# Two Mamba layers: C of every pair of states by DMA and a ScalarE copy to PSUM, where TensorE spread it from the rows of dbl

## The chip, the cores and the metric

The kernel runs on one core of a Trainium2 chip. The core's engines work side by side, each through its own list of instructions in order, and wait for each other by semaphores: TensorE (PE, with its weight loads as PEld), VectorE (DVE), ScalarE (ACT), GpSimd (POOL) and SyncE (SP), which here only issues DMAs. SBUF is the working memory of 128 partitions; PSUM holds what TensorE writes, and ScalarE and VectorE read and write it too. The metric is the time of one execution on the device, in microseconds (us), as the median of several executions.

## The reference

The network has four layers on x of shape (2, 128, 56, 56), each of them x + layer(group norm of x): an agent attention, a 3x3 convolution, a mixture of experts on 2x2 patches, and last a pair of Mamba blocks, one along each image row from left to right (f), one from right to left (b). The change lies in the Mamba blocks. Cut to what matters here:

```python
xz = x @ in_w.T;  xi, z = split(xz)                  # 256 channels each
xc = silu(conv_b + causal conv of xi with 4 taps)
dbl = xc @ xproj_w.T
dt, Bm, Cm = split(dbl, [8, 8 + 16])                 # 16 states
dt = softplus(dt @ dt_w.T + dt_b);  A = -exp(Alog)
# along the row, for every channel d and state s:
h[d, s] = exp(dt[d] * A[d, s]) * h[d, s] + dt[d] * xc[d] * Bm[s]
y[d] = sum over s of h[d, s] * Cm[s]
y = (y + xc * Dp) * silu(z);  result = y @ out_w.T
```

Both results are fused by one more matrix and normalized over the channels.

## The kernel before

The first three layers take the time up to about 1735 us and are not touched. The Mamba stage, `mamba_pair`, works on 14 blocks of 448 positions (8 image rows): 2 images, 7 blocks each. A block has two halves, f then b, and a half has 16 units. States go in pairs: pair j holds states 2j and 2j+1 in the lower and the upper 64 partitions. A pair has two units, m = 0 and 1, for the two groups of 128 channels; a unit holds its 128 channels as two runs r of 448 side by side, so that a tile is 128 partitions by 896. One unit consists of

- `decay`: two ScalarE activations write dA = exp(dt * A) to PSUM (L1820; two buffers);
- `push`: one GpSimd product, dBu = dtu * B (L1831; four buffers);
- `scan`: one VectorE scan along the rows, h = dA * h + dBu (L1853). After the second unit of a pair, one product over both units multiplies h by C, in place;
- `collect`: TensorE adds the two states of a pair into y with a matrix of two identities (L1873).

The product by C is done by GpSimd for the pairs 0, 3 and 6 of f and 0 and 3 of b (`POOLED`, L1440; the product is L1859), and by VectorE for the eleven others (L1862). Where GpSimd does it, C comes from SBUF: `send_low` writes the rows of B and C of a half (`low`, 40 rows: 8 of dt, 16 of B, 16 of C) to a DRAM buffer `far` and reads them back spread over 64 partitions each, B for all pairs (`Bs`) and C for the pooled pairs (`Cs`, one tile per direction). Where VectorE does it, `read_out` lets TensorE spread C: a column of the identity, broadcast to 64 columns, picks one row of `low` and writes it to 64 partitions of `c_ps`, a PSUM bank with the tag "c" of which there is one. Each of the two matmuls stands in the profile as two records, so a pair has four (L1841).

The order of the work is written out by hand. `units` lists all 448 units; the loop over them is a step each. In step n it issues `decay` of unit n+1; the fetches that were left by earlier stages (ScalarE copies out of PSUM); `push` of unit n+3; `scan` of unit n; `close` of a finished half (L1879, yv = y * silu(z)); `read_out` in the first unit of a pair that isn't pooled; `collect` of unit n-3, mostly; and then the stages that `book` put on this step: everything that prepares the next block (norm, conv, Silu, low, dt, softplus, weigh, the sends, the gates) and finishes the last one (fuse, the norm's statistics in `measure`, root, newton, normalize, turn_back, onto). A stage writes the bank "mm", or "c" where it is booked with that tag: f.low at step 15 of f, f.softplus(0) at step 6 of b, both softplus of b at the first two steps of the next f, conv(1) of b at step 12 of f. Places that the prediction speaks of, by their step n of a block (0 to 15 is f, 16 to 31 is b): the f Silu of the next block with the Silu of the gates at 10, the b Silu at 18 (two table loads and two activations each, L1884 to L1887), f.low at 15, b.send_steps at 11, f.send_steps at 27, fuse at 4, measure at 6.

The SP queue carries, in the order of the steps, `far`, `Bs`, `Cs`, the doubled copies `dtu` and `dt` of a half (`send_steps`, eight DMAs, L1808), and the result (L1688). `weigh` on GpSimd (L1793) makes dtu = dt * xc.

```python
units[0][0].decay(0)
for h, u in units[:3]:
    h.push(u)
for n, (h, u) in enumerate(units):
    if n + 1 < len(units):
        who, i = units[n + 1]
        who.decay(i)
    fetch(n)
    ...
```

## Time and profile before

| | |
|---|---|
| median of 5 executions | 3106.36 us (3105.32 to 3116.91) |
| profiled execution | 3105.2 us, span 3103.5 us |
| granted clock of TensorE, mean | 0.937 |
| Mamba stage, about 1735 us to the end | 1370 us |
| one block in its steady part | 95.2 us |
| L1831 dBu, GpSimd | 448 times 2140 ns |
| L1853 scan, VectorE | 448 times 2007 ns |
| L1862 product by C, VectorE | 154 times 2022 ns |
| L1859 product by C, GpSimd | 70 times 3991 ns |
| L1820 dA, ScalarE | 896 times 637 ns |
| L1841 c_ps, TensorE | 616 records, 172.9 us |
| L1873 y, TensorE | 1792 records, 469.1 us |
| Cs by DMA | 140 of 112 KB |

Times in the profile count from the start of the span. "PE" busy is modelled, since matmuls overlap; "PEclk" is the share of its full clock that TensorE was granted. A line of the timeline gives start, length, engine, source line, operation, output and inputs, how many instructions are merged into it, and in brackets the idle time before it and what ended it. A line of waits gives who waited for whom: total us, how often, the longest. A line of stretches gives, for each engine, its busy time with the number of instructions.

### The profile page before, as it was taken

The numbers are of one execution on the slowest core, as the hardware profiler recorded it, in microseconds if no ns is written. First come the engines' busy times: TensorE is split into PE (matmuls) and PEld (weight loads), VectorE is DVE, ScalarE is ACT, GpSimd is POOL, SyncE is SP. The second block draws the span as 40 slices with busy tenths as digits, with TensorE's granted clock in tenths as the row PEclk, the third lists the DMA queues.
The fourth block names the chain that finished last, engine by engine and source line by source line (L and its number), as shares of the span: only waits on it lengthen the run. The fifth ranks groups of instructions, "written<-read, shape, count | busy, mean of one in ns | idle before, by whom it ended". The sixth has DMA issues, their size and how long they took to land. (4 is left out here: it accounts for less than half of the span.)

```text
span 3103.5 us, 34608 instructions
## 1 busy us (share of the span) xinstructions
PE 2822.2 (91%) x12964; PEld 1076.8 (35%) x12964; DVE 2225.2 (72%) x2033; ACT 1758.6 (57%) x2634; POOL 1499.9 (48%) x801
## 2 busy tenths in 40 slices
PE   7999999999998899999996789999889998889885
PEld 3333333332344444444443322333323333233321
DVE  5879999999886111111112699999999999999996
ACT  5778788877641011111111577776777767777763
POOL 3000100100521000000002699999999999999995
PEclk9999999999998899999997888989989899999987
DMA  1000000000011878777773553444444535444440
GB/s 54 1 1 1 1 1 1 1 1 1 1 38 42 316 280 321 288 311 305 296 311 104 116 101 81 91 105 91 98 85 83 111 81 114 90 83 91 96 100 8
DMA packets 133271, 333.65 MB, mean 108 GB/s; under 512 B 20228, under 2 KB 90340, under 8 KB 129492
## 3 DMA queue, kind: packets, MB, share of 16 engines
q1 hardware_dynamic: 111104, 303.96, 34.0%
q0 software_dynamic: 5520, 15.62, 1.6%
q10 hardware_dynamic: 16452, 11.61, 1.2%
q8 instruction: 106, 1.74, 0.2%
q14 instruction: 89, 0.73, 0.1%
HBM read 262.56 MB, written 17.20 MB: 90 GB/s over the span
## 5 line engine op out<-in xcount | busy, mean ns | idle before, releaser
L1831 POOL TENSOR_TENSOR dBu<-dtu,Bs 128x896 f32<-128x896 f32 x448 | 944.9, 2140 | 50.9 <-DVE h L1853 38.1
L1853 DVE TENSOR_TENSOR_SCAN h<-dA,dBu 128x896 f32<-128x896 f32 x448 | 879.0, 2007 | 58.8 <-ACT dA L1820 46.2
L620 ACT ACTIVATE ex<-sc 128x896 f32<-128x896 f32 (+1 forms) x700 | 602.7, 917 | 124.6 <-PE sc L617 113.4
L627 DVE TENSOR_TENSOR ex_sum<-ex_sum,ex 128x1792 f32<-128x1792 f32 (+1 forms) x238 | 492.5, 2069 | 35.3 <-ACT ex L620 21.3
L1873 PE MATMUL y<-h,both 128*64 128x448 f32 x1792 | 469.1, 625 | 16.2 <-POOL h L1859 15.0
L617 PE MATMUL sc<-q,k 32*128 32x448 f32 (+1 forms) x2800 | 403.6, 587 | 3.6 <-ACT ex L620 2.9
L1341 PE MATMUL h_ps<-w,xs_c 128*128 128x512 f32 x896 | 393.0, 597 | 10.3 <-issue 10.3
L1820 ACT ACTIVATE dA<-dt,f_A 128x448 f32<-128x448 f32 x448 | 284.5, 637 | 107.1 <-DVE h L1853 76.4
L635 PE MATMUL av<-ex,va 128*32 128x448 f32 (+1 forms) x2800 | 334.3, 552 | 0.1
L1862 DVE TENSOR_TENSOR h<-h,c_ps 128x1792 f32<-128x1792 f32 x154 | 311.3, 2022 | 26.4 <-PE c_ps L1841 11.6
L582 POOL TENSOR_TENSOR a_e<-a_e,a_inv 112x784 f32<-112x784 f32 x14 | 41.6, 2973 | 583.9 <-ACT ex L620 394.5
L1820 ACT ACTIVATE dA<-dt,b_A 128x448 f32<-128x448 f32 x448 | 283.8, 636 | 66.8 <-DVE h L1853 53.6
L1345 DVE TENSOR_TENSOR he<-h_ps,sg 128x512 f32<-128x512 f32 x56 | 38.5, 691 | 381.4 <-PE h_ps L1341 344.4
L1289 POOL DMA_INDIRECT xr<-xd,whom x28 | 28.1, 1003 | 535.4 <-PE xr_ps L1331 489.7
L1859 POOL TENSOR_TENSOR h<-h,Cs 128x1792 f32<-128x1792 f32 x70 | 279.3, 3991 | 2.2 <-DVE h L1853 2.2
L1841 PE MATMUL c_ps<-low,ident 40*64 40x448 f32 x616 | 172.9, 642 | 89.6 <-DVE h L1862 67.4
L1341 PEld LDWEIGHTS h_ps<-w,xs_c 128*128 128x128 f32 x896 | 168.9, 191 | 218.3 <-issue 202.6
L1873 PEld LDWEIGHTS y<-h,both 128*64 128x64 f32 x1792 | 116.6, 150 | 319.8 <-issue 249.1
L617 PEld LDWEIGHTS sc<-q,k 32*128 32x128 f32 (+1 forms) x2800 | 137.7, 181 | 230.0 <-issue 132.3
L1362 PE MATMUL o_ps<-w,ht 128*128 128x512 f32 x448 | 197.2, 592 | 0.4 <-ACT ht L1357 0.4
L1344 ACT ACTIVATE sg<-h_ps 128x512 f32<-128x512 f32 x56 | 33.4, 597 | 256.5 <-PE h_ps L1341 256.5
L1364 ACT ACTIVATE ot<-o_ps,share 128x512 f32<-128x512 f32 x28 | 19.3, 688 | 278.9 <-PE o_ps L1362 278.9
(334 smaller groups left out, 3059.5 us busy)
## 6 DMA issues: line engine op xcount, KB each, us to landing
w<-in_L_conv_w_dram SPq DMA_DIRECT2D x28, 4096.0 KB, 19.3
w<-in_L_conv_w_dram SPq DMA_DIRECT2D x28, 2048.0 KB, 10.3
Bs<-far SPq DMA_DIRECT2D x56, 896.0 KB, 10.6
dtu<-sp_u SPq DMA_DIRECT2D x108, 224.0 KB, 3.9
dt<-dt SPq DMA_DIRECT2D x108, 224.0 KB, 5.2
Cs<-far SPq DMA_DIRECT2D x140, 112.0 KB, 7.5
os<-ot ACTq DMA_DIRECT2D x28, 256.0 KB, 7.8
xd<-xt SPq DMA_DIRECT2D x14, 224.0 KB, 2.8
```

Of the source, the lines that this page charges most:

```text
L617: nc.tensor.matmul(sc[:size, j, :BLK], self.m.k[rows, at : at + size], self.q[rows, :], start=True, stop=True)
L620: nc.scalar.activation(ex[:size, 2 * g : 2 * g + 2, :], sc[:size, :, :BLK], AF.Exp, scale=scale)
L627: nc.vector.tensor_add(self.total[g][:size], self.total[g][:size], ex[:size])
L635: nc.tensor.matmul(self.av[rows, :BLK], self.m.va[:size, i, rows], self.ex[i][:size, h, :], start=i == 0, stop=i == STEPS - 1,)
L1341: nc.tensor.matmul(h_ps, xc[:, q, :], w1[:, q, f0 : f0 + 512], start=q == 0, stop=q == 3)
L1362: nc.tensor.matmul(o_ps, ht[:, i, :], w2[:, i, :], start=i == 0, stop=i == nj - 1)
L1820: nc.scalar.activation(self.dA[u][:, r * BLK : (r + 1) * BLK], self.dt2[:, m, r, :], AF.Exp, scale=self.w.A[:, j, 2 * m + r : 2 * m + r + 1],)
L1831: nc.gpsimd.tensor_tensor(self.dBu[u], self.dtu2[:, m], self.B[:, j, :].unsqueeze(1).to_broadcast(shape), ALU.mult)
L1853: nc.vector.tensor_tensor_scan(hf, af, bf, 0.0, ALU.mult, ALU.add)
L1859: nc.gpsimd.tensor_tensor(h4, h4, c, ALU.mult)
L1862: nc.vector.tensor_tensor(h4, h4, c, ALU.mult)
L1873: nc.tensor.matmul(self.y[r * H : (r + 1) * H, m, :BLK], both, self.hc[j][:, m, r, :], start=False, stop=j == PAIRS - 1)
```

## The change

C comes by DMA for every pair, not only for the pooled ones. `send_low` sends B alone. A new `send_c(j)` sends C of one pair into a tile of 128 by 448, of which five rotate for both directions together; it is called six units ahead of use, and for the first three pairs before the loop. `read_out` is one ScalarE copy of that tile to `c_ps` in place of TensorE's matmuls, and it stands earlier in the step: after the fetches, before `push`, `scan` and the booked stages. GpSimd's product reads the pair's tile in place of a slice of the old one.

```diff
-                self.C = work.tile([P, len(pooled), BLK], F32, name="Cs", tag=f"Cs{self.w.d}", bufs=1)
                 for s in range(2):
                     half = slice(s * H, (s + 1) * H)
                     src = far[:S, :].rearrange("(j s) t -> s j t", s=2)
                     nc.sync.dma_start(self.B[half], src[s].unsqueeze(0).to_broadcast([H, PAIRS, BLK]))
-                    for n, j in enumerate(pooled):
-                        r = S + 2 * j + s
-                        nc.sync.dma_start(self.C[half, n, :], far[r : r + 1, :].to_broadcast([H, BLK]))
+            def send_c(self, j):
+                self.C[j] = work.tile([P, BLK], F32, name="Cs", tag="Cs", bufs=5)
+                for s in range(2):
+                    r = S + 2 * j + s
+                    nc.sync.dma_start(
+                        self.C[j][s * H : (s + 1) * H, :], self.far[r : r + 1, :].to_broadcast([H, BLK])
+                    )
...
             def read_out(self, u):
-                r = R + S + u // 2 * 2
                 self.c_ps = ps.tile([P, 512], F32, name="c_ps", tag="c")
-                for s in range(2):
-                    one_row = net.ident[:LOW, r + s : r + s + 1].to_broadcast([LOW, H])
-                    nc.tensor.matmul(self.c_ps[s * H : (s + 1) * H, :BLK], one_row, self.lo, start=True, stop=True)
+                nc.scalar.copy(self.c_ps[:, :BLK], self.C[u // 2])
...
+            for h, u in units[:6:2]:
+                h.send_c(u // 2)
             units[0][0].decay(0)
             for h, u in units[:3]:
                 h.push(u)
...
                 fetch(n)
+                if u % 2 == 0 and not h.by_pool(u):
+                    h.read_out(u)
+                if u % 2 == 0 and n + 6 < len(units):
+                    who, i = units[n + 6]
+                    who.send_c(i // 2)
                 if n + 3 < len(units):
                     who, i = units[n + 3]
                     who.push(i)
                 h.scan(u)
                 if done:
                     done.pop().close()
-                if u % 2 == 0 and not h.by_pool(u):
-                    h.read_out(u)
```

## The prediction

> **What bounds the kernel now.** I read the page's busy shares and slices first: the change lies in the last stage, the Mamba layers, from about 1735 us on. Then the busy times of that stage alone.

> ```profile
> PE 2822.2 (91%) x12964; PEld 1076.8 (35%) x12964; DVE 2225.2 (72%) x2033; ACT 1758.6 (57%) x2634; POOL 1499.9 (48%) x801
> ```

> ```profile
> 1800.00:3000.00 1200.00, 1082.68 (x3700) 370.15 (x3696) 1132.70 (x776) 879.51 (x1449) 1161.37 (x529) 0.91 0.46 94
> ```

> The second line's columns after the length are PE, PEld, VectorE, ScalarE, GpSimd, the granted clock, the DMA share and GB/s. VectorE is busy 94% and GpSimd 97%, so little can be won. Which of the two sets the pace is told by the waits of that stage:

> ```profile
> DVE h L1853 <- ACT dA L1820: 41.0, 38, 2.0
> DVE h L1862 <- PE c_ps L1841: 6.1, 13, 0.9
> DVE sp_e L1775 <- ACT dt_ps L1769: 2.8, 6, 1.3
> ...
> DVE h L1853 <- POOL dBu L1831: 0.6, 1, 0.6
> ```

> ```profile
> POOL dBu L1831 <- DVE h L1853: 31.8, 34, 2.2
> ```

> VectorE waits for GpSimd once; GpSimd waits for VectorE 34 times. So VectorE paces, and its waits for ScalarE and TensorE are the time that can change. A block takes 95.2 us (the residual adds of L1686 start at 2320.28, 2415.46 and 2510.93), and there are 13 blocks in which the next one is prepared. The timeline puts VectorE's waits at fixed places of each block: 0.2 to 0.9 before the first product of the f half (for c_ps), 0.84 at the f Silu, 1.98 at the b Silu, about 0.5 before b's last pair. The largest, on ScalarE and then VectorE:

> ```profile
> 2465.19 0.53 ACT L1735 COPY low<-low_ps 40x448 f32<-40x448 f32 x1 [1.26 <-PE low_ps L1732]
> 2465.62 1.30 ACT L1820 ACTIVATE dA<-dt,b_A 128x448 f32<-128x448 f32 x2
> ...
> 2470.34 0.55 ACT L1769 ACTIVATE dt_ps<-sp_e 128x448 f32<-128x448 f32 x1
> 2470.91 1.28 ACT L1884 ACT_TABLE_LOAD   x1
> ...
> 2475.30 1.31 ACT L1820 ACTIVATE dA<-dt,b_A 128x448 f32<-128x448 f32 x2
> ```

> ```profile
> 2476.71 3.94 DVE L1853 TENSOR_TENSOR_SCAN h<-dA,dBu 128x896 f32<-128x896 f32 x2 [1.98 <-ACT dA L1820]
> ```

> From the copy of low at 2465.19 to dA at 2475.30 ScalarE runs without a pause, so whatever comes into that chain, or delays its head, is paid in full. The head is TensorE's low_ps, which starts when VectorE's product of pair 7 (2461.38 to 2463.40) frees the bank "c".

> ```profile
> 2400.86:2404.27 3.41, 2.19 (x8) 0.56 (x10) 3.31 (x3) 3.23 (x7) 3.35 (x3) 1.00 0.14 31
> 2404.27:2407.68 3.41, 3.41 (x12) 0.77 (x8) 3.41 (x3) 0.93 (x2) 3.41 (x3) 0.50 1.01 234
> ...
> 2465.71:2469.12 3.41, 3.13 (x15) 1.08 (x14) 3.41 (x3) 3.34 (x7) 3.41 (x3) 1.00 0.20 25
> 2469.12:2472.53 3.41, 1.32 (x8) 0.20 (x4) 3.31 (x3) 3.35 (x6) 3.41 (x2) 1.00 1.00 222
> ```

> The clock fell after the first and the fourth, not after the third. If each matmul's time is weighted with its contracted rows over 128 (8 for dt_ps, 40 for c_ps, else about 128), the first has 0.30 of a window, the fourth 0.31, the third 0.54. Over all windows of the stage that began at full clock, every one up to 0.47 was followed by half clock and none from 0.48; from half clock it rose again from 0.81 on, never at 0.79 or less.

> [...] The window that ends at 2404.27 held 2.19 us of matmuls, so the trace decides for a load limit.

> **The change, part by part.** Removed: 308 matmuls of c_ps, 616 records, 0.90 us of TensorE per pair. Added: 154 ScalarE copies, and Cs by 448 DMAs in place of 140, 34 MB more.

> *VectorE and GpSimd* run the same instructions; their products stay at 2.02 and 3.99 us. Nothing.

> *The price of a copy.* SBUF to PSUM, 128x448: between the copy of low (next instruction 0.43 after it starts) and L1769 (0.55). I take 0.45. The copy waits for the product of the pair before (bank "c") and for two DMAs; behind it on ScalarE stand the step's later stages and the next dA, for which VectorE's scan waits. That dA waits anyway for a scan which comes after the same product. Eleven copies per block; ScalarE is idle 27% of the stage, and behind nine of them the next dA has a pause or at least 1.4 us before its scan. Two stand in the Silu chains:

> - b Silu, pair 1: in the unbroken chain above. +0.45 x 13 = +5.9. Its own product at 2471.18 then starts 0.3 later, hidden under the longer wait for dA.
> - f Silu, pair 5: before, ScalarE took xc at 2351.69 only when TensorE's conv was done, and Silu began at 2352.34. Without c_ps of pair 4 the conv ends 0.9 earlier; the copy then waits for the product that ends at 2351.34, and Silu begins at about 2351.95. -0.4 x 13 = -5.2.

> *First product of the f half.* c_ps was ready 1.07 after the dt copy that freed its bank; the ScalarE copy is ready 0.45 after it. The 13 waits of 6.1 in sum vanish: -6.1. The dt_ps waits (2.8) shrink, since TensorE no longer stops for c_ps ahead of dt_ps: -2.0.

> *Start of the stage.* Six Cs DMAs (0.67 MB) stood ahead of the first dtu and dt while the DMA engines were 99% busy at 211 GB/s, 3.2 us; now they follow. The first Silu can come 2.0 earlier (it is then held by conv_ps, done at 1735.15, where xc was taken at 1737.22). Next, 1.75 of c_ps ahead of dt_ps goes out of VectorE's wait of 1.99 for dt_ps: 1.7. At the first f Silu the conv comes 0.9 earlier and the copy costs 0.45: 0.5. Bounds 0 and -6; I take the sum, -4.2.

> *SP.* The send of pair b0 reuses the buffer of f3, and so waits for GpSimd's product (2440.44 to 2444.43). Behind it in the queue is b's send_steps, until now issued at 2438.16. It moves to 2445.7 (two issues, 1.27): dtu is issued by 2448.5, lands after 3.9, and is wanted at 2455.61; the last dt, issued about 2450.7, lands after 5.2, at 2455.9, and dA wants it at 2459.40. Cover 3.5 us or more: nothing. If a dt took the 11.8 of the slowest Cs, it would cost 3.1 a block, 40 in all. Copies have their Cs 17 us ahead of use against landings of 7.4. f's send_steps has the send of f0 ahead of it, released by GpSimd's product at 2396.2, 6 us before its own start at 2402.49. The 34 MB raise the stage's DMA share from 0.46 to some 0.6.

> *TensorE's clock.* With c_ps gone its work closes up and leaves longer pauses. Ahead of low_ps (lines of 2459 on):

> ```profile
> 2459.40 0.97 PE L1841 MATMUL c_ps<-low,ident 40*64 40x448 f32 x4 [1.00 <-ACT xc L1712]
> 2460.30 0.97 PE L1873 MATMUL y<-h,both 128*64 128x448 f32 x4
> 2461.20 1.03 PE L1720 MATMUL gate_ps<-pad,b_gate_t 128*128 128x448 f32 x2
> 2462.16 0.97 PE L1873 MATMUL y<-h,both 128*64 128x448 f32 x4
> 2463.46 1.32 PE L1732 MATMUL low_ps<-xc,f_xp_t 128*40 128x448 f32 x3 [0.32 <-DVE h L1862]
> ```

> The y and gate ahead now start at 2456 and end by 2458.9; the y of 2462.16 needs GpSimd's product, done at 2461.69. That is 2.8 us of nothing, and 0.6 more before low_ps. Nearly every position of the grid then has a window under 0.475 that ends between 2460.7 and 2464.0, so low_ps runs partly at half clock. It took 1.67 at full clock (2486.28) and 3.21 at half (1740.15). Bounds 0 and +1.54; I take 1.1, as the half clock begins or ends inside it: +14.3.

> The second place is between sp_ps and f's skip: without the two c_ps near 2425 and 2428 there are pauses of 1.9 and 1.0 with one gate (0.95) between. About half of the positions fall under the limit, and skip, fuse and conv then run late by 1.2 to 2.9 us. The norm's statistics on VectorE have 0.75 of margin behind fuse, and conv ends just in time for Silu. Bounds 0 and +2.7 a block; I take 0.78 as the mean: +10.1.

> [...]

> Sum: -4.2 - 6.1 - 5.2 - 2.0 + 5.9 + 14.3 + 10.1 = +12.8. The profiled execution took 3105.2 (span 3103.5), so 3118; the median shown, 3106.4, lies 1.2 above it.

> **The rivals.**

> *The clock holds.* If the last two terms are nothing, the sum is -11.6: 3094, faster. It decides at 0.475 of a window: TensorE's own work would have to stay spread out as now. For it: low_ps never ran at half clock before. Against it: c_ps itself weighs only 0.08 of a window, but its waits are what spread the rest.

> *Half of it.* low_ps slows, skip does not, or the other way: +2.7 or -1.5, about 3104 to 3108. Within 0.2% (6.2 us), which is about what can be told from no change.

> *A late transfer or a crowded ScalarE.* dt behind the queue on SP, up to +40 as above; or the copies cost 0.45 not twice but four to six times a block, +12 to +23. 3130 to 3158. Against it: the cover shown.

> **How the numbers follow.** Forecast 0.52, its own range 3111 to 3135. Clock holds 0.24, half of it 0.13, late transfer or crowded ScalarE 0.11. Faster 0.24, same 0.13, slower 0.52 + 0.11 = 0.63. The range goes from the clock rival's 3094, less 2, to 3140; below lies about half of that rival's spread, 0.1, above most of the last one.

> **What would show it.** Right: VectorE's wait at the b Silu grows from 1.98 to about 3.5, low_ps shows matmuls of about 1 us, the granted clock of the stage falls under 0.91, no wait for c_ps is left, the f Silu wait is about 0.5 in the blocks where skip is fast. Wrong: if low_ps stays at 0.54 a matmul, the sum falls to the first rival; if ScalarE or GpSimd waits for Cs or dt, to the last.

## The result, and the profile after

The changed kernel takes 3114.14 us (median of 26 executions, 3106.93 to 3120.47); the kernel before, run beside it, 3109.32 us (median of 50). The ratio is 1.0014, with a 95% interval of 1.0008 to 1.0021: slower, by about 4.4 us. The forecast was slower by 12.8. The profiled execution took 3109.71 us, with a span of 3107.9.

Line numbers move with the diff: dA is now L1822, the copy to c_ps L1840, the scan L1852, the product by C on VectorE L1861 and on GpSimd L1858, skip L1868, y L1872, the b Silu L1883 to L1886.

The busy times of the page, and the stretch from 1800 to 3000 us (PE, PEld, VectorE, ScalarE, GpSimd, granted clock, DMA share, GB/s):

```profile
PE 2685.4 (86%) x12348; PEld 1057.9 (34%) x12348; DVE 2225.5 (72%) x2033; ACT 1824.8 (59%) x2788; POOL 1499.2 (48%) x801
```

```profile
1800.00:3000.00 1200.00, 957.69 (x3131) 351.24 (x3132) 1128.65 (x773) 935.90 (x1583) 1155.01 (x526) 0.88 0.54 119
```

TensorE has 125 us less to do in this stretch, ScalarE 56 more, and the granted clock went from 0.91 to 0.88: TensorE does less and is granted less. The waits of VectorE and of GpSimd between 1800 and 3060:

```profile
DVE h L1852 <- ACT dA L1822: 43.4, 38, 2.2
DVE h L1852 <- issue: 7.0, 12, 0.8
DVE h L1861 <- ACT c_ps L1840: 6.4, 13, 1.3
DVE h L1852 <- POOL dBu L1833: 0.7, 1, 0.7
...
POOL dBu L1833 <- DVE h L1852: 38.7, 31, 2.0
```

VectorE still paces. Its waits for c_ps by TensorE (6.1) and for dt_ps (2.8) are gone, and 13.4 us of new waits stand in their place: 0.4 to 0.8 a block ahead of the scans of b's pair 1 (the "issue" row, for which the profile names no releaser; the dA that stands behind the copy of low ends 0.1 ahead of the first of them), and 0.42 a block for the copy of pair 1 of b. Both lie in the b Silu chain, where the largest wait also went from 1.98 to 2.24. TensorE, then ScalarE, then VectorE there:

```profile
2460.79 1.76 PE L1872 MATMUL y<-h,both 128*64 128x448 f32 x4 [3.07 <-POOL h L1858]
2462.62 1.86 PE L1732 MATMUL low_ps<-xc,f_xp_t 128*40 128x448 f32 x3
...
2464.31 0.54 PE L1732 MATMUL low_ps<-xc,f_xp_t 128*40 128x448 f32 x1
```

```profile
2464.89 0.53 ACT L1735 COPY low<-low_ps 40x448 f32<-40x448 f32 x1 [1.44 <-PE low_ps L1732]
...
2470.51 0.52 ACT L1840 COPY c_ps<-Cs 128x448 f32<-128x448 f32 x1
2471.05 1.28 ACT L1883 ACT_TABLE_LOAD   x1
...
2475.45 1.31 ACT L1822 ACTIVATE dA<-dt,b_A 128x448 f32<-128x448 f32 x2
```

```profile
2471.07 2.02 DVE L1861 TENSOR_TENSOR h<-h,c_ps 128x1792 f32<-128x1792 f32 x1 [0.42 <-ACT c_ps L1840]
...
2476.86 3.94 DVE L1852 TENSOR_TENSOR_SCAN h<-dA,dBu 128x896 f32<-128x896 f32 x2 [2.24 <-ACT dA L1822]
```

The pause of 3.07 us ahead of y is there, y and the first part of low_ps run at half clock (y 1.76 where four records took 0.97), and the copy of low comes 2.62 us after the product that frees its bank, on the mean of 12 blocks, where it came after 1.79. The copy of C then takes 0.54 from start to start. Together the scan behind the b Silu comes 14.59 us after that product, before 13.34.

A block takes 95.60 us on the mean of the 11 steady ones (the distances of the residual adds), before 95.25. The last block's end is 1.6 us longer: the last y is at half clock (2.99, where the same eight records took 1.72), and VectorE waits 3.09 for it, before 1.83; a wait of 0.47 ahead of its last product by C is new as well.

```profile
3081.26 2.99 PE L1872 MATMUL y<-h,both 128*64 128x448 f32 x8 [3.09 <-DVE h L1861]
3084.29 1.09 DVE L1878 TENSOR_TENSOR yv<-y,zs 128x896 f32<-128x896 f32 x1 [3.09 <-PE y L1872]
```

### The profile page after: what moved, and what is told of

It is laid out like the page before. It is cut to its first block, busy times and chain, and to the rows that moved or that the text cites. A ratio compares the mean times of both kernels' runs of the same rounds, so it can differ in the third digit from the quotient of the medians.

```text
span 3107.9 us, 34183 instructions
## 1 busy us (share of the span) xinstructions
PE 2685.4 (86%) x12348; PEld 1057.9 (34%) x12348; DVE 2225.5 (72%) x2033; ACT 1824.8 (59%) x2788; POOL 1499.2 (48%) x801
## 3 DMA queue, kind: packets, MB, share of 16 engines
q1 hardware_dynamic: 135744, 339.30, 38.1%
q8 instruction: 101, 1.65, 0.2%
## 5 line engine op out<-in xcount | busy, mean ns | idle before, releaser
L1852 DVE TENSOR_TENSOR_SCAN h<-dA,dBu 128x896 f32<-128x896 f32 x448 | 880.1, 2007 | 64.9 <-ACT dA L1822 49.2
L1872 PE MATMUL y<-h,both 128*64 128x448 f32 x1792 | 482.6, 638 | 68.6 <-POOL h L1858 59.3
L1861 DVE TENSOR_TENSOR h<-h,c_ps 128x1792 f32<-128x1792 f32 x154 | 311.3, 2022 | 27.4 <-ACT c_ps L1840 12.5
L1822 ACT ACTIVATE dA<-dt,f_A 128x448 f32<-128x448 f32 x448 | 284.0, 636 | 77.2 <-DVE h L1852 50.4
L1822 ACT ACTIVATE dA<-dt,b_A 128x448 f32<-128x448 f32 x448 | 283.6, 635 | 59.3 <-DVE h L1852 47.4
L1858 POOL TENSOR_TENSOR h<-h,Cs 128x1792 f32<-128x1792 f32 x70 | 279.0, 3985 | 0.2 <-issue 0.2
L1872 PEld LDWEIGHTS y<-h,both 128*64 128x64 f32 x1792 | 125.3, 152 | 355.6 <-issue 217.8
L625 DVE TENSOR_TENSOR ex_sum<-ex 128x1792 f32<-128x1792 f32 x56 | 114.4, 2043 | 54.5 <-ACT ex L620 54.4
```

The source lines that it names most:

```text
L1822: nc.scalar.activation(self.dA[u][:, r * BLK : (r + 1) * BLK], self.dt2[:, m, r, :], AF.Exp, scale=self.w.A[:, j, 2 * m + r : 2 * m + r + 1],)
L1852: nc.vector.tensor_tensor_scan(hf, af, bf, 0.0, ALU.mult, ALU.add)
L1858: nc.gpsimd.tensor_tensor(h4, h4, c, ALU.mult)
L1861: nc.vector.tensor_tensor(h4, h4, c, ALU.mult)
L1872: nc.tensor.matmul(self.y[r * H : (r + 1) * H, m, :BLK], both, self.hc[j][:, m, r, :], start=False, stop=j == PAIRS - 1)
```

## The experiments

The theory of the prediction: with c_ps gone TensorE's load in some windows of 3.413 us falls under the limit that was read from the trace of before (weighed by rows, up to 0.47 of a window the clock fell, from 0.48 on it held), and low_ps (and, in some blocks, skip and fuse) run at half clock. The grid of 3.413 us stands in the clock records of the two traces: all 93 changes of the granted clock in the kernel before, and all 145 in the changed kernel, lie whole multiples of 3.41333 us apart, to 0.004 us. The rivals: the time comes from the order of ScalarE's work alone, or from the transfers. After the first runs a sharper form was on record as theory B: a block is drawn to 28 windows of the grid, 28 x 3.413 = 95.57 us, so that what is won at one place is given back at another.

The main readings in one place (`low_eight` and the probes on VectorE are in their own sections). "Block" is the mean distance of the residual adds, "low" the start of the copy of f's low after the product that frees its bank, "chain" the start of the scan behind the b Silu after the same product, "f Silu" VectorE's wait ahead of the scan behind the f Silu, all in us. These four are means over the blocks of one execution, the profiled one, which lies 4 us under its kernel's median for before and changed, 5 under for `b1_tensor` and 4 above for `no_tail`. The ratio is of all executions, against the kernel before run beside them.

| kernel | ratio to before, 95% interval | block | low | chain | f Silu |
|---|---|---|---|---|---|
| before | 1 | 95.25 | 1.79 | 13.34 | 0.80 |
| changed | 1.0014 [1.0008, 1.0021] | 95.60 | 2.62 | 14.59 | 0.64 |
| dma_alone | 0.9994 [0.9983, 1.0004] | 95.25 | 1.79 | 13.34 | 0.81 |
| b1_tensor | 1.0014 [1.0002, 1.0026] | 95.61 | 2.52 | 14.04 | 1.04 |
| low_full | 1.0037 [1.0023, 1.0052] | 96.38 | 2.87 | 14.84 | 0.58 |
| low_ten | 1.0010 [1.0000, 1.0020] | 95.73 | 1.86 | 13.83 | 0.81 |
| skip_eight | 1.0001 [0.9992, 1.0011] | 95.59 | 2.86 | 14.83 | 0.41 |
| both_places | 0.9994 [0.9985, 1.0003] | 95.58 | 2.10 | 14.08 | 0.41 |
| all_parts | 0.9957 [0.9943, 0.9971] | 94.39 | 1.85 | 13.38 | 0.41 |
| no_tail | 0.9957 [0.9943, 0.9970] | 94.68 | 2.47 | 13.99 | 0.41 |

### The transfers alone

`dma_alone`: the changed kernel, and TensorE still spreads C.

```diff
 def read_out(self, u):
     self.c_ps = ps.tile([P, 512], F32, name="c_ps", tag="c")
-    nc.scalar.copy(self.c_ps[:, :BLK], self.C[u // 2])
+    r = R + S + u // 2 * 2
+    for s in range(2):
+        one_row = net.ident[:LOW, r + s : r + s + 1].to_broadcast([LOW, H])
+        nc.tensor.matmul(self.c_ps[s * H : (s + 1) * H, :BLK], one_row, self.lo, start=True, stop=True)
```

> The changed kernel with all its transfers and their order, but every pair not taken by GpSimd is spread by TensorE as before, so that those C tiles arrive and are not used. Theory (the transfers cost nothing once they are under way, the loss is the clock and the copy): low_ps of the f half 540 ns, the b Silu chain as in the kernel before (13.3 us from the last scan ahead to the second behind), no new wait for a DMA on ScalarE or GpSimd; ratio 0.998 to 1.000, the start of the stage 2 us earlier included. Rival (the 34 MB more or the moved send of the steps cost time): GpSimd or dA waits for dt or dtu in each block, 0.3 us or more a block, ratio 1.001 or above with a full clock.

Measured 0.9994, the interval across 1. The stretch and VectorE's waits, 1800 to 3060:

```profile
1800.00:3000.00 1200.00, 1083.27 (x3700) 370.71 (x3700) 1132.93 (x777) 879.64 (x1450) 1154.75 (x529) 0.91 0.55 120
```

```profile
DVE h L1858 <- ACT dA L1822: 40.3, 38, 2.0
DVE h L1867 <- PE c_ps L1844: 6.2, 13, 1.0
```

The DMA share is that of the changed kernel (0.55, there 0.54, before 0.46), the clock and the waits are those of the kernel before, the chain is 13.34 to the hundredth. In the steady blocks the 34 MB and the new order on SP cost nothing that can be seen. Nor did they win the 2 us at the start of the stage that were expected: from the last adds of the stage ahead (which lie up to 1.5 us apart in these three executions) to the first residual add it took 215.05 us, before 215.24, in the changed kernel 213.37. They had won 1.4 by VectorE's second wait for dt_ps of the first b half (its sp_e comes 38.1 after the last adds, before 39.5), and lost it right behind that, where sp_ps of this half met a window at half clock. The kernel before, then `dma_alone`:

```profile
1764.33 1.02 PE L1785 MATMUL sp_ps<-sp_u,ident 128*128 128x448 f32 x2 [2.98 <-ACT sp_u L1780]
1766.89 0.53 ACT L1786 COPY dt<-sp_ps 128x448 f32<-128x448 f32 x1 [1.02 <-PE sp_ps L1785]
```

```profile
1762.73 1.86 PE L1787 MATMUL sp_ps<-sp_u,ident 128*128 128x448 f32 x2 [2.98 <-ACT sp_u L1782]
1766.72 0.53 ACT L1788 COPY dt<-sp_ps 128x448 f32<-128x448 f32 x1 [2.45 <-PE sp_ps L1787]
```

### Load ahead of low_ps: the clock, and how rows count

Small matmuls of 64 columns, into the columns 448 to 512 of the bank of the b gate, which nobody reads, issued behind that gate and ahead of y and low_ps.

```diff
+            def fill(self, n, w):
+                for _ in range(n):
+                    nc.tensor.matmul(self.gate_ps[:, BLK:], w, w[:, :64], start=True, stop=True)
...
 book(at + 46, lambda b=b: b.gate(1), late=1)
+book(at + 46, lambda b=b: b.fill(22, b.w.gate[:, 0, :]))
```

`low_full` is as shown; `low_eight` has `b.w.dt_t[:, 0, :]` there, which contracts 8 rows.

> The changed kernel, with 22 small matmuls (128 contracted rows, 64 columns, about 2.5 us in all) issued ahead of the low projection of each f half, in the pause before it, into bank columns that nobody reads. Theory (the clock): the load keeps the clock full, so the f low_ps matmuls fall from a mean of 706 ns back to about 540, the copy of low comes about 1.8 us after the product that frees the bank in place of 2.6, the first scan behind the b Silu comes 0.8 sooner in each of 12 blocks, and the kernel is about 10 us faster than the changed one: 3.0 to 6 us faster than the kernel before, ratio 0.997 to 0.999. Rival (the order of work on ScalarE or the bank alone sets that time): low_ps still starts when the product ends and the copy waits as it does now; ratio 1.001 as for the changed kernel, or more, by the matmuls added.

> As the run with 22 added matmuls of 128 contracted rows, but these contract 8 rows, so they take TensorE as long and weigh a sixteenth. Theory (the load is weighted with the contracted rows): 2.5 us of them count 0.05 of a window, the clock falls as in the changed kernel, low_ps of the f half stays near 700 ns, ratio 1.001 to 1.002. Rival (busy time counts, whatever the rows): the clock holds, low_ps 540 ns, the time is that of the run with 128 rows, 0.997 to 0.999.

Neither ratio is what the theory gave, but the times were no test: 22 of them take 5.02 us and not 2.5, and 6.28 in the block of `low_eight` below, where the clock halves under them, so both kernels hold low_ps back and come out 0.4% and 2.1% slower than the kernel before (`low_eight` has 1.0210 [1.0191, 1.0229]). The matmuls of low_ps themselves answer the question. The group of f in the 12 blocks with added matmuls (min/median/max in ns), `low_full` first:

```profile
L1737 PE MATMUL low_ps<-xc,f_xp_t x48: 539/539/539, 1888.3 to 2949.5; 128*40 128x448 f32 x48
```

```profile
L1737 PE MATMUL low_ps<-xc,f_xp_t x48: 540/954/954, 1896.9 to 3008.2; 128*40 128x448 f32 x48
```

After 22 back-to-back matmuls of 128 rows all 48 records are at full clock; after 22 of 8 rows the median is 954. In one of those blocks the 22 begin at full clock, at 2391.82, and run without a pause to 2398.1. The stretches (columns as above) show the clock fall under them:

```profile
2392.10:2395.51 3.41, 3.41 (x33) 3.41 (x33) 3.31 (x3) 3.35 (x8) 3.41 (x2) 1.00 0.01 2
2395.51:2398.00 2.49, 2.49 (x13) 2.39 (x12) 2.49 (x2) 1.60 (x4) 2.49 (x2) 0.51 0.25 92
```

TensorE was busy for the whole window of 3.41 us, and the clock halved at its end, as it did after the five other windows of this run that began at full clock and were filled by these matmuls. Weighed by their 8 rows of 128, these 3.41 us come to 0.06 of a window. So it is the load weighed by rows that goes with the clock here, and not the busy time alone, as the prediction had read from the windows. The trace of the changed kernel shows the same: of its windows from 1735 us on that began at full clock, the 64 behind which it fell come to 0.43 or less by rows, and the 236 behind which it held to 0.45 or more, a little below the prediction's 0.475; by busy time those that fell go up to 0.56 and those that held down to 0.45.

### Pair 1 of b back on TensorE: the copy in the chain

```diff
+if self.w.d == "b" and u == 2:
+    r = R + S + u // 2 * 2
...
+    return
 nc.scalar.copy(self.c_ps[:, :BLK], self.C[u // 2])
```

> The changed kernel, but pair 1 of each b half is spread by TensorE as before, all others are copied. Theory (that copy stands in the unbroken chain on ScalarE behind the b Silu): the chain loses one copy, the first dA behind the Silu and its scan come 0.45 to 0.55 sooner in each block, VectorE's wait of 0.42 for c_ps there goes; 12 blocks, 5 to 7 us less than the changed kernel, ratio 0.999 to 1.000. c_ps fits on TensorE in its pause of 4.9 us and costs nothing. Rival (what the copy takes is only idle time of ScalarE, since the low projection's clock sets the chain): no change, ratio 1.001 to 1.002.

Theory and rival were each half right. The chain lost 0.55 us (14.59 to 14.04), the price of one copy, and the wait for c_ps there is gone:

```profile
2466.65 0.55 ACT L1771 ACTIVATE dt_ps<-sp_e 128x448 f32<-128x448 f32 x1
2467.22 1.28 ACT L1889 ACT_TABLE_LOAD   x1
...
2471.62 1.31 ACT L1822 ACTIVATE dA<-dt,b_A 128x448 f32<-128x448 f32 x2
```

And yet the ratio stayed 1.0014 and the block 95.61. It was given back at the f Silu, where VectorE now waits 1.04 in all 11 blocks, in the changed kernel in four of them, because f's skip runs at half clock each time (2.79 where it takes 1.77 at full clock), and fuse and conv follow it:

```profile
2328.69 2.79 PE L1874 MATMUL y<-xc,f_skip 128*128 128x448 f32 x4 [0.19 <-DVE yv L1884]
```

```profile
2353.52 7.77 DVE L1858 TENSOR_TENSOR_SCAN h<-dA,dBu 128x896 f32<-128x896 f32 x4 [1.04 <-ACT dA L1822]
```

That the block came out at 95.6 again, from a chain half a microsecond shorter, gave theory B.

### One place filled, and the other

`low_ten` has 10 matmuls ahead of low_ps in place of 22. `skip_eight` has 8 of them ahead of the b gate and the f skip, and none ahead of low_ps:

```diff
+book(at + 34, lambda f=f: f.fill(8, f.w.gate[:, 0, :]))
 book(at + 35, lambda b=b: b.gate(0))
```

> As the run with 22 added matmuls of 128 rows ahead of the f low projection, with 10: 22 took 5.0 us and pushed the projection back, 10 take 2.3 us and end inside the pause of 3.07 us. Theory A (the clock costs, and costs only there): f low_ps 540 ns, its copy 1.8 us after the freeing product and the scan behind the b Silu 13.8 (both as far as the copy alone allows), blocks 0.8 us shorter than the changed kernel's 95.6, so 94.8; 9 us less in all, ratio 0.998 to 0.999. Theory B (the block locks to 28 windows of the clock's grid, 95.57 us: what is won at one place moves the pauses against the grid until another place is hit): low_ps 540 ns too, but skip and fuse run at half clock in every block, the f Silu's wait is 1.04 instead of 0.41 in every block, blocks 95.4 to 95.6, ratio 1.000 to 1.001. Rival (the order on ScalarE alone): chain 14.6 as in the changed kernel.

> The changed kernel with 8 small matmuls (128 rows, 64 columns, 1.8 us) in the pause of 2 us ahead of the b gate and the f skip, and none ahead of the low projection. Skip and fuse then stay at full clock, the f Silu's wait is 0.41 in every block. Theory A (places are independent): low_ps as in the changed kernel, mean copy 2.6 after the product; 4 or 5 blocks become 0.6 shorter, 2.5 to 3 us in all, ratio 1.000 to 1.001. Theory B (locked to 28 windows): the f low projection loses more than now, its copy comes 2.8 to 3.3 after the product in every block, blocks stay 95.5 to 95.6, ratio 1.001 to 1.002.

`low_ten`, the group of low_ps, and a block (2316 to 2412):

```profile
L1737 PE MATMUL low_ps<-xc,f_xp_t x48: 539/539/542, 1886.1 to 2938.7; 128*40 128x448 f32 x48
```

```profile
2329.01 2.84 PE L1873 MATMUL y<-xc,f_skip 128*128 128x448 f32 x4 [0.28 <-DVE yv L1883]
```

low_ps is at full clock in every block and the chain 13.83, as both theories had it: 0.76 less than in the changed kernel. That shows what the clock takes from the chain. But the block is 95.73, its median 95.62. Seven of the 11 blocks pay 1.04 at the f Silu behind a slow skip, and the other four pay 1.26 to 1.32 at a third place that no theory had named (see `both_places`). The ratio, 1.0010 [1.0000, 1.0020], is that of theory B and above that of A; B's slow skip in every block came in seven of 11.

`skip_eight`: the f Silu's wait is 0.41 in every block, and now low_ps loses more:

```profile
L1737 PE MATMUL low_ps<-xc,f_xp_t x48: 539/886/954, 1889.2 to 2942.5; 128*40 128x448 f32 x48
```

The copy of low comes 2.68 to 2.98 after the product, the block takes 95.59. The trace says theory B; the ratio, 1.0001 [0.9992, 1.0011], lies in A's range and doesn't exclude B's 1.001.

### Both places, and one copy less

> Both sets of added matmuls, 10 ahead of low_ps and 8 ahead of skip. Both theories: no fall of the clock costs at either place, low_ps 540 ns, f Silu wait 0.41, chain behind the b Silu 13.8; nothing is left to lock to, blocks 94.6 (the 95.25 of before, +0.45 for the copy in the chain, -0.43 at the f Silu, -0.5 for c_ps, -0.15 for dt_ps); 11 us less than the changed kernel: ratio 0.997 to 0.999, faster than the kernel before. If a block still takes 95.5 or more, the clock isn't what the change lost by.

Measured 0.9994 and blocks of 95.58: the expectation failed, and by its last sentence the clock would be acquitted. It isn't. The sentence took for granted that there were two places only. In seven of the 11 blocks VectorE now waits 1.25 to 1.38 for the copy of C of f's first product on VectorE, which stands on ScalarE behind the copy of dt, which waits for sp_ps of the b half at half clock:

```profile
2127.72 1.86 PE L1792 MATMUL sp_ps<-sp_u,ident 128*128 128x448 f32 x2 [0.82 <-DVE h L1866]
2129.38 1.70 PE L1792 MATMUL sp_ps<-sp_e,minus 128*128 128x448 f32 x2
...
2413.52 1.02 PE L1792 MATMUL sp_ps<-sp_u,ident 128*128 128x448 f32 x2 [1.60 <-DVE h L1866]
```

```profile
2136.07 0.53 ACT L1793 COPY dt<-sp_ps 128x448 f32<-128x448 f32 x1 [2.38 <-PE sp_ps L1792]
2136.63 0.54 ACT L1845 COPY c_ps<-Cs 128x448 f32<-128x448 f32 x1
```

```profile
2137.20 2.02 DVE L1866 TENSOR_TENSOR h<-h,c_ps 128x1792 f32<-128x1792 f32 x1 [1.26 <-ACT c_ps L1845]
```

The third line of the first fence is the same sp_ps in another block, at full clock; there is no such wait in that block. The added matmuls don't always hold the clock either: in that block and the one ahead of it the copy of low came 3.37 and 3.25 after the product. The shortest block, which paid at none of these places, took 94.53 us, the longest 96.00: that their mean is 95.58 again is in part chance. The shortest block of the kernel before took 94.46, and of `dma_alone` 94.50.

`all_parts` adds the spread of b's pair 1 by TensorE, and 11 matmuls ahead of the last y; `no_tail` leaves those 11 out.

> Both sets of added matmuls, pair 1 of each b half spread by TensorE as before, and 11 added matmuls in the pause of 3 us ahead of the last output's matmuls at the end. Theory (each cost is separate once the clock holds): the chain behind the b Silu 13.3 as in the kernel before, blocks 94.1; the wait for the last y 1.8 instead of 3.1; 17 us less than the changed kernel, ratio 0.995 to 0.997. Rival (the copy's half microsecond is hidden also when the clock holds): the time of the run with both sets alone, 0.997 to 0.999, less 1.3 us at the end.

> The run with all parts, without the 11 added matmuls at the end: there the clock was already at half, they took 4.96 us and held the last y back by 1.7 to 2. All theories: the wait for the last y returns from 5.1 to 3.0 to 3.4, 2 us less than with them, ratio 0.994 to 0.996; most blocks 94.0.

Ratios 0.9957 and 0.9957, 13 us faster than the kernel before, in the range expected for both. No run put added matmuls into the kernel before, so how much of the 13 us the change itself gives is open. The chain is 13.38 wherever low_ps is at full clock, and the shortest blocks take 93.9. The 11 matmuls at the end won nothing, and the trace of `all_parts` shows why: the clock was already at half there, they took 4.96 us, and VectorE waited 5.09 for the last y; without them 3.35. The 2 us that `no_tail` was to gain by that can't be told from a ratio whose interval is 8 us wide. In its profiled execution, 4 us above its median, five blocks take 95.2 to 95.7, because low_ps runs at half clock there although the matmuls stand ahead of it: two short pauses behind them (0.57 and 0.74 in one block) lie in a window after which the clock falls. In that of `all_parts` two blocks are long (95.1 and 95.5), by the slow sp_ps.

Those windows also fit a weight of these matmuls of 64 columns below their time. Weighed as in the prediction, by the time and rows of each matmul record, the five that end ahead of a slow low_ps come to 0.61 or 0.62 of a window, well above its limit of 0.475, and two others of the same weight held the clock. If the added matmuls are counted at half their time, the five come to 0.450 to 0.461, and every window of this run with added matmuls behind which the clock held to 0.466 or more. The two slow low_ps of `both_places` fit too: 0.61 and 0.62 by time, 0.47 and 0.45 so counted.

The stretch and VectorE's waits of `no_tail`:

```profile
1800.00:3000.00 1200.00, 1011.01 (x3688) 405.44 (x3688) 1139.15 (x789) 938.94 (x1582) 1159.63 (x533) 0.90 0.55 121
```

```profile
DVE h L1863 <- ACT dA L1827: 33.7, 36, 2.1
DVE h L1863 <- POOL dBu L1838: 11.6, 9, 2.1
```

The second row doesn't say that GpSimd now paces. Seven of its nine waits, 10.7 of the 11.6 us, lie in the five blocks with a slow low_ps: five of 1.27 to 1.34, in which dBu had been done for 0.4 us or more when the scan began and dA for 0.09, and two of 2.1 at the b Silu, where dA and dBu ended within 0.1 of each other. In `all_parts` VectorE waits 37.6 for dA and 0.9 for dBu.

### Detuning: a probe that was not what it seemed

If the grid holds a block at 95.57, extra work on VectorE should be free up to that point. One useless product per block was to be that work:

```diff
 nc.vector.tensor_mul(self.yv, self.y[:, :, :BLK], self.zs)
+if self.w.d == "b":
+    for _ in range(1):
+        nc.vector.tensor_mul(self.zs[:, 0, :], self.zs[:, 0, :], self.zs[:, 1, :])
```

`no_tail_plus` has it on top of `no_tail`, `plus_one` on top of the changed kernel, `plus_three` three of them.

> The same kernel (two sets of added matmuls, pair 1 of each b half by TensorE) with one useless product of 128x448 on VectorE after each output of a b half, about 0.55 us (128x896 from PSUM takes 1.08) in each of 12 blocks, where VectorE doesn't wait. Rival (each block is a sum of its parts): blocks 94.55 in place of 94.0, 6.6 us more in all, ratio 0.997. Theory B (locked to 28 windows where the shortfall to 95.57 is less than the 1.27 that the slowed sp_ps can cost): 94.55 needs 1.02, so it locks, as the run with both sets did; most blocks become 95.5 to 95.7, 13 to 18 us more in all, ratio 0.999 to 1.001, three times what the added work takes.

> The changed kernel with the same useless product of about 0.55 us on VectorE in each block. Rival (sum of the parts): blocks 96.1 in place of 95.6, 6.6 us more than the changed kernel, ratio 1.0035. Theory B (locked): the block at full clock would be 94.5 to 95.1 with the product, still under 95.57, so the pauses move against the grid, less of low_ps or skip is slowed, and blocks stay 95.5 to 95.7; 0 to 1 us, ratio 1.001 to 1.002, the b low copy 2.0 to 2.4 after the freeing product in place of 2.62, or f Silu waits of 0.41 alone.

> The changed kernel with three such products, 1.65 us in each block. Rival (sum of the parts): blocks 97.25, 20 us more than the changed kernel, ratio 1.008. Theory B: a block at full clock takes 96.15, more than 28 windows, so nothing can hold it at 95.57; blocks lie between 96.15 and 97, 7 to 16 us more than the changed kernel, ratio 1.0035 to 1.0065, and their half-clock windows fall at changing places.

All three missed: ratios 1.0104 [1.0087, 1.0122], 1.0134 [1.0116, 1.0153] and 1.0216 [1.0202, 1.0230], blocks 98.31, 98.90 and 100.73. The product costs not 0.55 but up to 3.96 us (`no_tail_plus`). In `plus_three`, its group (min/median/max ns):

```profile
L1881 DVE TENSOR_TENSOR zs<-zs x36: 624/626/3853, 1857.9 to 2970.1; 128x448 f32<-128x448 f32 x36
```

In `plus_one`, GpSimd and VectorE around one of them:

```profile
2149.82 6.26 POOL L1833 TENSOR_TENSOR dBu<-dtu,Bs 128x896 f32<-128x896 f32 x3
```

```profile
2153.08 3.48 DVE L1881 TENSOR_TENSOR zs<-zs 128x448 f32<-128x448 f32 x1
```

It ends 0.5 us after GpSimd's unbroken row of products (2156.56 against 2156.08). In all 13 blocks of `plus_one` in which GpSimd is at work it ends 0.48 after the end of one of GpSimd's products: in nine after the last of the row, in four, where it takes 1.8, after the one before the last. Of the three in a row in `plus_three` the first is long in nine of 13 blocks, the first two in the other four, and the rest, with no product of GpSimd beside them, take 0.62. So the added work pushed every block past 95.57, and the question was not put. In `no_tail_plus` it even hid the third place: a block that waited 1.39 for c_ps had a shorter useless product behind it and took 98.0 like its neighbours. The grid's hold on the block is therefore a pattern that four kernels with different work show (changed, b1_tensor, skip_eight, both_places: 95.58 to 95.61), with the place of the loss seen in each; that it would pull a block with more work on VectorE back to the same length was not settled. Counted from an edge of the grid in windows of 3.4133 us, the residual adds of the steady blocks lie at 0.51 to 0.62 of a window in all 12 of `b1_tensor` and at 0.67 to 0.80 in 11 of 12 of the changed kernel, while in `all_parts` they are spread from 0.11 to 0.93.

## Why the prediction was right and wrong

The sign was right, and so were the causes it named: slower, by TensorE's clock and by the copy in the b Silu chain, against the gain of c_ps off TensorE. The size was a third of the forecast, 4.4 against 12.8, and within the 0.2% that it had called about what can be told. What came lies nearest to the rival that it gave 0.13, "half of it": low_ps slows, skip does not, +2.7. The point, 3118, was of a profiled 3105.2, and that profile came to 3109.71. That the median, 3114.14, lies inside the forecast's own 3111 to 3135 is luck: the kernel before took 3109.32 beside it, 3.0 more than the median that the prediction started from, and 3106.36 x 1.0014 is 3110.7. Step by step, measured over the 11 or 12 steady blocks of the profiled executions:

| step | predicted | measured |
|---|---|---|
| start of the stage | -4.2 | -1.9 |
| first product of f | -6.1 | -5.2 (0.47 a block to 0) |
| f Silu | -5.2 | -4.3 (0.39 x 11), skip apart |
| dt_ps | -2.0 | -2.8 |
| copy in the b Silu chain | +5.9 | +5.0 (0.42 x 12) |
| half clock in low_ps | +14.3 | +10.0 (0.83 x 12) |
| half clock at skip, fuse, conv | +10.1 | +2.5 (0.63 in 4 blocks) |
| end of the last block | none | +1.6 |
| SP, transfers | 0 | 0 (dma_alone) |

The sum is +4.9. The last residual add came 4.8 later than before, but 1.3 of that was there when the stage began, so the stage itself took 3.5 more; the kernel before lost about 1 us in one block (96.3 long, half clock at b's low projection) that the changed kernel did not, and that no step of the table holds. That a table of two single executions comes near the 4.4 of the medians is partly luck.

- *The clock in low_ps* is shown: with enough load ahead, all its records return to 539 ns and the chain loses 0.76 (`low_ten`); with matmuls of 8 rows it stays slow (median 954, `low_eight`). The term was mis-sized: 1.1 was taken, 0.83 measured, since only y and the first part of low_ps fell under the slow window.
- *The copy in the chain* measured 0.42, and 0.55 where it was taken out (`b1_tensor`), against 0.45.
- *Skip, fuse and conv* is the step that failed. It took about half of all grid positions, as if a block could stand anywhere on the grid, for 0.78 a block. The blocks did not stand anywhere: at 95.60 they are nearly 28 windows long, kept nearly one position, and only four of 11 met a slow skip, at 0.63. Adding the two clock terms as if they were independent was the error behind it. `low_ten` and `skip_eight` show it: with one place filled the block pays more at the other.
- *The start* was a sum of three savings, and most of it was there at first: the scan behind the first f Silu begins 59.4 after the last adds of the stage ahead, before 63.0. On the way, sp_ps of the first b half ran at half clock as in `dma_alone` (the copy of dt waits 2.47 for it, before 1.02), and VectorE's product behind it waited 5.01 for the copy of C, before 3.37 for TensorE; in `dma_alone`, where TensorE spreads C, the same product waits 4.80, so ScalarE's copy isn't what made this wait long. About 1.7 of these 3.6 were lost again by the first residual add: 0.8 in the first b Silu chain (13.96, before 13.14; the table's 12 blocks don't hold this one), 0.6 at the first product of the next f half (1.29, before 0.73); the rest is open. The part laid to the transfers was worth 1.4 until the clock took it (`dma_alone`), and 0.2 in the end.
- *The end* was overlooked: with c_ps gone from the last half, its last y runs at half clock (2.99 where the same records took 1.72).
- *The 11.6 us that would be won if the clock held* were not reached by any run with all the copies. As a sum against the kernel before, as it ran, no run shows them wrong: the shortest block of `both_places`, where none of the named places was slowed, took 94.53, 0.72 less than the mean before, and 13 times that with the start's 1.9 is 11.3 (an estimate from one block). But the gain isn't TensorE's work. The savings were taken from waits that were themselves longer by half clock: the first product of f waited 0.22 in some blocks of the kernel before and 0.8 to 0.9 in others, and in one of these the twelve y ahead of sp_ps took 4.71, at half clock nearly to their end, where they took 4.17 in one with the short wait. The shortest block of the kernel before took 94.46. If these two blocks are taken as the bases, one each and the second with added matmuls, the change is worth nothing in the steady blocks, and its loss is that a block pays 1.1 us to the clock on the mean where it paid 0.8.
- VectorE as the pace, no late transfer, and no new wait for the transfers of Cs or dt came out as said. Of the signs, low_ps at up to 954 ns, the stage's clock at 0.88 and the f Silu's wait of 0.41 behind a fast skip came. Two did not: the wait at the b Silu went to 2.24 and not to 3.5 (with the two new waits ahead of it, 0.58 and 0.42 on the mean, 3.24), and waits for c_ps are left, 6.4 us of them, now by ScalarE.

## What to carry over

Taking work off an engine that isn't the bound can cost time through its clock: here TensorE had 125 us less to do in 1200, its granted clock went from 0.91 to 0.88, and the kernel became 4.4 us slower. Before removing matmuls, see in the trace behind which windows the clock fell and what load they held, and price the matmuls there at what they take then (a record of low_ps 954 ns, at full clock 539). In this loop, whose block of 95.6 us lies near 28 windows of 3.413, gains and losses at single places didn't add up (`b1_tensor`: the chain 0.55 shorter, the block 95.61 where it was 95.60): price the block with all its slowed places at once, and take as its base the shortest block seen in the trace rather than the mean (94.46 and 95.25 in the kernel before). Here a few useless matmuls of full rows in the pauses, together with one pair left on TensorE, make the changed kernel 13 us faster than the kernel before (0.9957), where the change alone is 4.4 slower; the same matmuls in the kernel before were not tried.

## What was not expected of the hardware

- The block length stayed at 95.58 to 95.61 in four kernels whose b Silu chains run from 14.04 to 14.83 us; 28 windows of 3.413 are 95.57. Single blocks lie at 95.42 to 95.78 in `b1_tensor`, but at 95.17 to 96.07 in the changed kernel and 94.53 to 96.00 in `both_places`.
- A product of 128x448 on VectorE with both inputs in SBUF took up to 3.96 us beside GpSimd's products (`no_tail_plus`), and 0.62 when GpSimd had none running (`plus_three`). In nine of 13 blocks of `plus_one` it ended only 0.48 us after the last of an unbroken row of GpSimd's products (in the block shown it lasted through two more of 2.1 us), and in four 0.48 after the one before the last. The product by C, four times as wide and with one input in PSUM, took 2.02 throughout. Whether the place of the inputs makes this difference was not shown: no run tried the product with C in SBUF.
- 22 matmuls of 64 columns took 5.02 us, 0.23 each at full clock, where 0.11 had been expected. In the load that holds the clock a weight of about half of that time fits the windows of `no_tail` (so counted, 0.461 and less fell, 0.466 and more held).
